# Cross-attention over eight batches: one addition of P1, one half's statistics and two sums of weights at other places of the order

## The chip, the core and the metric

The kernel runs on one core of a Trainium2 chip. The metric is device time in microseconds (us), the median of three runs. The engines are TensorE (PE in the profile, with PEld for its weight loads), VectorE (DVE), ScalarE (ACT), GpSimd (POOL) and SyncE (SP), which issues nearly all the transfers. Each engine works through its own queue in order.

## The reference, cut to what matters

Eight batches of 256 rows of 1024 numbers attend to 256 keys each, with 32 heads of 32 numbers. Keys and values are the same context.

```python
xn = (x - mean(x)) * rsqrt(var(x) + 1e-5) * gamma + beta
Q = heads(xn @ Wq.T); K = V = heads(ctx)
probs = softmax(where(mask, Q @ K.T / sqrt(32), -inf))
out = x + merge_heads(probs @ V) @ Wout.T
```

Everything is in float32.

## The kernel before, in words

**Slots.** The work is cut into 64 head groups, eight per batch, each of four heads. The main loop (from L937 on) has one pass per group; a pass is called a slot here. In slot n TensorE makes the scores of group n+1 (L963) and the products with the values of group n-2 (L973); VectorE, ScalarE and GpSimd make the softmax of group n+1 (`softmax_parts`, L512 to L618). So slot 9 holds the softmax of group 10. Beside these, each slot has a hand-placed share of other work.

**The softmax.** For each of four heads VectorE adds the mask to the scores and reduces them (L524), ScalarE takes the exponential and its sum (L528), VectorE makes the reciprocal (L535), GpSimd, VectorE or ScalarE scale by it (L543, L538), VectorE transposes the blocks (L549), ScalarE copies half of them aside (L555), and SyncE moves them into the tile pT (L614, L618). Points in the softmax take "hooks": evacuations of other products. The hook called "soon" comes behind the second head's reductions, hook 0 behind the fourth's.

**The output product.** Attention times Wout is done for batch b in slots 8(b+1) to 8(b+1)+8 by a Strassen-like scheme of seven half-size products: A11 by B11 (its result is called P1), A12 by B21, S2 by T2, S3 by T3, A22 by T4, S1 by T1, S4 by B22. Each has four steps of TensorE (L720; each step shows as two matmuls), given out by the table STEPS: in slot 9 seven steps, in slot 10 one behind the values and two behind the softmax, and so on; step 23, the last of S1 by T1, is the only one in slot 15 that comes right behind the values, and two more come later in that slot. A, the halves of the attention, are summed to S by GpSimd (`sum_at`, L696); the halves B of Wout are summed to T once, for all batches, chunk by chunk (`sum_wo`, L182). Accumulators are in PSUM: P1 in one bank, the sums that follow in another. ScalarE copies P1 out (`keep_p1`, L728). For each of the four quarters of the output GpSimd adds P1 to the residual r (`add_p1`, L753), and VectorE adds what stands in PSUM (`take`, L758, or `store`, L762, which also sends the result). The first quarter's store, r plus the result of A12 by B21, has to have read its bank before the S2 steps of TensorE begin in it.

**The query product.** Batches 0 and 1 make their queries directly; from batch 2 on (L447) there is the same scheme, with sums of the normalised x (`sum_x`, L435) and of Wq (`sum_wq`, L396: T1, T2, T3 and T4, each in four chunks, built once in slots 6 to 14). Batch 2's products stand in slots 10 to 16, one a slot: S1, S4, A11, S2 (with T2, slot 13), S3 (with T3), A22 (with T4, slot 15), A12. Batch 3's begin in slot 18.

**Layer norm.** For batch 3 the two halves of rows have their statistics (`ln_stats`: two BN statistics, L227, their aggregate, L230, and an addition, L232, on VectorE, then a power on GpSimd, L235) in slots 8 and 9, their normalisation (GpSimd's shift, L245, and ScalarE, L248) in slots 10 and 11, their block transposes (L316) in slots 11 and 12, and their moves by SyncE (L332) in slots 12 to 14. In slots above 8 the statistics come behind the softmax on VectorE, and the power is put off to a list called `later`.

**GpSimd's order in a slot** is: its parts of the softmax, S2's sum (when it is due), shift, the other sums of attention, sums of x, additions of P1 in slots 11 to 13, the powers of `later`, folds of Wq (early slots), and last `sums[n]`, the slot's sums of weights. In `sums[n]` the sums of Wout entered at L853 come first, then those of Wq (L858), then Wout's T1 (L860).

Of the kernel before, what the change touches and what calls it, by code (L numbers as in the profile page):

```python
# [59 lines left out]
def xattn_kernel(  # L60
# [101 lines left out]
    B11, B21, B22, T1, T2, T3, T4 = range(7)  # L162
# [201 lines left out]
    def fold(o):  # L364

        nc.gpsimd.tensor_tensor(
            wq[:, o], wq[:, o], gs.unsqueeze(2).to_broadcast([P, NC, P]), ALU.mult
        )
# [9 lines left out]
    SPLIT = 2  # L378
# [295 lines left out]
    def steps_of(b):  # L674
        if b == B - 2:
            return ENDS
        return STEPS
# [73 lines left out]
    def add_p1(b, s, h):  # L751
        r = rs[b, s, h]
        nc.gpsimd.tensor_tensor(r, r, p1s[b], ALU.add)  # L753
# [46 lines left out]
    for n in range(N):  # L800
# [12 lines left out]
    loads, stats, norms, trans, moves, biases, masks = (  # L813
        {n: [] for n in range(N)} for _ in range(7)
    )
    for b in range(1, B):
        first = NQ * (b - 1) + 2
        if b == 1:
            when = dict(moves=())
        elif b == 2:  # L820
            when = dict(
                loads=(0, 1), stats=(2, 3), norms=(3, 4), trans=(4, 5),
                moves=tuple(5 + (i + 2) // 6 for i in range(16)),
            )
        else:
            when = dict(
                loads=(first - 12, first - 11) if b == SPLIT + 1 else (first - 13, first - 12),
                stats=(first - 10, first - 9) if b == SPLIT + 1 else (first - 11, first - 9),
                norms=(first - 8, first - 7), trans=(first - 7, first - 6),
                moves=tuple(first - 6 + (i + 2) // 6 for i in range(16)),  # L830
            )
        for table, key in (
            (loads, "loads"), (stats, "stats"), (norms, "norms"), (trans, "trans"),
        ):
            for i, n in enumerate(when.get(key, ())):
                assert n < first
                table[n].append((b, i))
        for n in range(N):
            part = [i for i, slot in enumerate(when["moves"]) if slot == n]
            if part:  # L840
                assert n < first - 1
                moves[n].append((b, part))
        biases[NQ * b - 2].append(b)
        if b % 2 == 0:
            masks[NQ * b - 7].append(b)


    sums = {n: [] for n in range(N)}
    for n, which, *chunks in (
        (0, T3, 0), (1, T3, 1), (2, T2, 0), (3, T2, 1), (4, T3, 2, 3), (5, T2, 2, 3),  # L850
        (6, T4, 0, 1), (8, T4, 2), (11, T4, 3),
    ):
        sums[n] += [partial(sum_wo, which, c) for c in chunks]  # L853
    for n, which, *chunks in (
        (6, "T1", 0), (7, "T1", 1, 2, 3), (8, "T2", 0), (9, "T2", 1), (10, "T2", 2), (11, "T2", 3),
        (11, "T3", 0), (12, "T3", 1, 2), (13, "T3", 3), (13, "T4", 0), (14, "T4", 1, 2, 3),
    ):
        sums[n] += [partial(sum_wq, which, o) for o in chunks]  # L858
    for n, *chunks in (12, 0, 1), (13, 2), (14, 3):
        sums[n] += [partial(sum_wo, T1, c) for c in chunks]  # L860


# [33 lines left out]
    for c in range(NC):  # L896
        copy_x0(1, c, nc.scalar if c < NC // 2 else nc.vector)
    first = softmax_parts(0, (partial(copy_q, 1), partial(copy_q, 2)), (), (), {}, [
        partial(ln_stats, 1, 0), partial(ln_stats, 1, 1),
        partial(ln_norm, 1, 0, nc.vector),  # L900
    ])
# [16 lines left out]
    for b in range(B - 1):  # L918
        done, ends = 0, b == B - 2
        for i, counts in enumerate(steps_of(b)):  # L920
            n = NQ * (b + 1) + i
            for place, k in enumerate(counts):
                steps.setdefault((n, place), []).append((b, range(done, done + k)))
                done += k
        for i, *what in (
            ((2, keep_p1), (3, take_po_q), *((i, copy_po, i) for i in range(3, 8))) if ends else
            ((1, keep_p1), (2, add_p1, 0, 0), (2, store, 0, 0), (3, take, 0, 1), (4, take, 1, 1), (6, store, 1, 0),
             (7, store, 1, 1), (8, store, 0, 1))
        ):
            evacuations[NQ * (b + 1) + i].append((what[0], b, *what[1:]))  # L930
# [6 lines left out]
    for n in range(N):  # L937
        b, i = divmod(n - NQ, NQ)
# [109 lines left out]
            make_q(halves[n], second=True, chunks=range(NC // 2))  # L1048
        if n + 2 < NQ:
            fold(n + 2)  # L1050
        for one in sums[n]:
            one()
        if N - NQ + 2 < n < N - 1:
# [106 lines left out]
```

## Time and profile before

| what | us |
|---|---|
| median of three runs | 571.01 (570.69 to 571.02) |
| the profiled execution | 571.32 |
| its span, first to last instruction | 569.5 |
| TensorE busy | 561.8 |
| VectorE, ScalarE, GpSimd busy | 468.5, 423.7, 394.0 |

The granted TensorE clock is 1.00 throughout, and HBM gives and takes 137 GB/s over the span. The starts of slots, taken from the first score matmul of each in TensorE's timeline, are: slot 9 at 89.14, 10 at 97.50, 11 at 107.48, 12 at 116.84, 13 at 125.35, 14 at 133.86, 15 at 142.37, 16 at 152.26, 17 at 159.90, 18 at 168.27.

How to read it: a group's line gives the code line, the engine, the operation, out<-in, and a count. In a timeline the first two numbers are the start and the duration in us, and a bracket at the end gives the engine's idle time before the instruction and what ended it. In the waits view a line says who waited for whom, then the total in us, the number of waits and the longest. In the table by stretches a row gives the stretch, its length, each engine's busy time with its count of instructions, the granted clock, the DMA share and GB/s. The ends of matmuls are modelled, so starts are the firmer numbers.

### The profile page before, as it was taken

How to read it: one execution, taken by the hardware profiler on the slowest of the kernel's cores; microseconds unless marked ns; L12 is line 12 of the kernel's file. 1: busy time of each engine (PE TensorE's matmuls, PEld its weight loads, DVE VectorE, ACT ScalarE, POOL GpSimd, SP SyncE). 2: the span in 40 equal slices, each digit the busy share in tenths (PEclk: the TensorE clock that was granted, in tenths of full speed). 3: DMA queues.
4: the chain of work that ended last, by engine and by line, in shares of the span. 5: the costliest groups of instructions: out<-in, count | busy, mean ns of one | idle time of the engine just before them, and what ended most of it. 6: DMA issues, size and time to landing. Idle time of an engine off the chain costs nothing.

```text
span 569.5 us, 20200 instructions
## 1 busy us (share of the span) xinstructions
PE 561.8 (99%) x7266; PEld 393.9 (69%) x7266; DVE 468.5 (82%) x1716; ACT 423.7 (74%) x1464; POOL 394.0 (69%) x636
## 2 busy tenths in 40 slices
PE   8999999999999999999999999999999999999997
PEld 7888886667667777667776777667866767755454
DVE  5979889899888888979898888988888878779923
ACT  3699999898668858787667867778767776769920
POOL 2688887899687565866569566677648657448780
PEclk9999999999999999999999999999999999999999
DMA  8966677756798667867788857887658874536751
GB/s 306 397 174 204 179 199 223 252 176 174 219 305 247 202 177 198 289 203 214 195 243 227 226 166 211 261 246 202 185 142 253 251 202 133 146 103 182 216 157 74
DMA packets 47219, 119.02 MB, mean 209 GB/s; under 512 B 8976, under 2 KB 9744, under 8 KB 47120
## 3 DMA queue, kind: packets, MB, share of 16 engines
q1 hardware_dynamic: 46976, 117.74, 69.8%
q8 instruction: 57, 0.93, 0.8%
q14 instruction: 42, 0.34, 0.2%
q10 hardware_dynamic: 144, 0.01, 0.0%
HBM read 66.33 MB, written 11.53 MB: 137 GB/s over the span
## 4 chain that ended last, share of the span: by engine, by line
PE 80%; POOL 7%; DVE 5%; ACT 3%; issue 3%; DMA 1%; SPq 0%; DVEq 0%; POOLq 0%; ACTq 0%
PE po_S L720 20%; PE pq_A L447 18%; PE pv L636 10%; PE sc L486 10%; PE po_A L720 10%; PE pq_S L447 7%; PE po_end L787 3%; ACT e L528 2%; POOL e L543 2%; DVE e L524 2%; DVE pT L549 1%; PE po_last L787 1%; POOL wq L396 1%; POOL wo L182 1%; DMA pT<-pT 1%
## 5 line engine op out<-in xcount | busy, mean ns | idle before, releaser
L543 POOL TENSOR_SCALAR e<-e,rden 128x256 f32<-128x256 f32 x466 | 215.3, 478 | 128.7 <-DVE rden L535 126.1
L528 ACT ACTIVATE e<-e,mn 128x256 f32<-128x256 f32 x512 | 254.1, 502 | 47.4 <-DVE mn L524 46.3
L549 DVE STREAM_TRANSPOSE pT<-e 128x512 f32<-128x512 f32 x256 | 179.0, 704 | 35.6 <-POOL e L543 26.2
L524 DVE CUSTOM_DVE_ANT_0 e<-sc,mb 128x256 f32<-128x256 f32 x512 | 185.4, 416 | 27.0 <-PE sc L486 26.7
L555 ACT COPY pc<-pT 128x512 f32<-128x512 f32 x128 | 79.0, 617 | 55.2 <-DVE pT L549 34.9
L528 ACT ACTIVATION_READ_ACCUMULATOR e<-e,mn 128x1 f32 x512 | 98.6, 193 | 0.0
L486 PEld LDWEIGHTS sc<-k,qa 32*128 32x128 f32 x1024 | 46.2, 184 | 42.1 <-issue 20.1
L720 PE MATMUL po_S<-wo,at 128*128 128x512 f32 x152 | 74.3, 606 | 0.0
L636 PE MATMUL pv<-pT,v 64*32 64x128 f32 x4096 | 74.1, 274 | 0.0
L486 PE MATMUL sc<-k,qa 32*128 32x256 f32 x1024 | 73.6, 401 | 0.1
L636 PEld LDWEIGHTS pv<-pT,v 64*32 64x32 f32 x4096 | 57.0, 105 | 22.5 <-issue 12.4
L720 PE MATMUL po_A<-wo,at 128*128 128x512 f32 x128 | 59.4, 605 | 0.0
L345 PE MATMUL pq<-xnT,wq 128*128 128x256 f32 (+1 forms) x240 | 55.0, 384 | 0.0
L447 PEld LDWEIGHTS pq_A<-xnT,wq 128*128 128x128 f32 x416 | 48.5, 192 | 6.2 <-issue 5.0
L720 PE MATMUL po_S<-wo,s 128*128 128x512 f32 x104 | 50.2, 607 | 2.5 <-POOL wo L182 1.3
L345 PEld LDWEIGHTS pq<-xnT,wq 128*128 128x128 f32 x240 | 44.6, 190 | 8.2 <-issue 1.5
L447 PE MATMUL pq_A<-xnT,wq 128*128 128x128 f32 x416 | 48.5, 275 | 0.0
L535 DVE RECIPROCAL rden<-den 128x2 f32<-128x2 f32 x256 | 38.3, 150 | 7.7 <-ACT e L528 6.5
L524 DVE DVE_READ_ACCUMULATOR2_ANT mn<- 128x1 f32 x512 | 42.6, 83 | 0.0
L720 PEld LDWEIGHTS po_A<-wo,at 128*128 128x128 f32 x128 | 23.0, 190 | 25.6 <-issue 24.4
L720 PEld LDWEIGHTS po_S<-wo,at 128*128 128x128 f32 x152 | 25.5, 190 | 19.5 <-issue 19.5
L753 POOL TENSOR_TENSOR r<-r,p 128x512 f32<-128x512 f32 x24 | 30.6, 1275 | 5.0 <-DMA r<-in_x_dram 4.0
(102 smaller groups left out, 665.8 us busy)
## 6 DMA issues: line engine op xcount, KB each, us to landing
v<-in_kv_dram SPq DMA_DIRECT2D x32, 512.0 KB, 4.1
pT<-pT SPq DMA_DIRECT2D x128, 128.0 KB, 3.3
pT<-pc SPq DMA_DIRECT2D x128, 128.0 KB, 4.1
ring<-kept_T SPq DMA_DIRECT2D x20, 512.0 KB, 5.3
k<-in_kv_dram SPq DMA_DIRECT2D x32, 256.0 KB, 4.0
x<-in_x_dram SPq DMA_DIRECT2D x15, 512.0 KB, 5.9
r<-in_x_dram SPq DMA_DIRECT2D x28, 256.0 KB, 4.6
out_dram<-r SPq DMA_DIRECT2D x28, 256.0 KB, 3.5
```

The costliest lines, as they stand in the source:

```text
L345: nc.tensor.matmul(pqs[n], wq[:, o, c, :], xnTs[b](c), start=(c == 0), stop=(c == NC - 1),)
L447: nc.tensor.matmul(pqs[b][:, o, :], w[:, c], x_[:, c], start=begins and o + c == 0, stop=c == NK - 1, skip_group_check=True,)
L486: nc.tensor.matmul(scs[n][j][:, s, :], qa[r, n % NQ, ts(s, P)], ks[n - n % 2][r, n % 2, :], start=True, stop=True,)
L524: nc.vector.tensor_tensor_reduce(out=e[:, s, :], in0=pss[j][:, s, :], in1=mbs[n // NQ], scale=1.0, scalar=NO_SCORE, op0=ALU.add, op1=ALU.m ...
L528: nc.scalar.activation(e[:, s, :], e[:, s, :], AF.Exp, bias=mn[:, s : s + 1], scale=-1.0, accum_out=den[:, s : s + 1],)
L535: nc.vector.reciprocal(rden, dens[j])
L543: engine.tensor_scalar(es[j][:, s, :], es[j][:, s, :], rden[:, s : s + 1], 1.0, ALU.mult, ALU.mult,)
L549: nc.vector.transpose(pT[:, :, :, j, :, :].rearrange("p a i s k -> p (a i) s k"), es[j].rearrange("p s (b t) -> p b s t", t=K),)
L555: nc.scalar.copy(pc[:, :, ts(j, 2)], pT[:, 1, :, ts(j, 2)])
L636: nc.tensor.matmul(pvs[n][r][j * HD : (j + 1) * HD], vs[n - n % 2][ts(r, 2 * K), i, ds(n % 2 * P + j * HD, HD)], pT[ts(r, 2 * K), :, i, j, ...
L720: nc.tensor.matmul(po, operand(b, name)[:, c], wo[:, which, c], start=begins and c == 0, stop=c == NK - 1, skip_group_check=not begins,)
L753: nc.gpsimd.tensor_tensor(r, r, p1s[b], ALU.add)
```

## The change

```diff
-                stats=(first - 10, first - 9) if b == SPLIT + 1 else (first - 11, first - 9),
+                stats=(first - 10, first - 8) if b == SPLIT + 1 else (first - 11, first - 9),
...
+    sums[14].append(partial(sum_wo, T1, 3))
     for n, which, *chunks in (
-        (6, "T1", 0), (7, "T1", 1, 2, 3), (8, "T2", 0), (9, "T2", 1), (10, "T2", 2), (11, "T2", 3),
+        (6, "T1", 0), (7, "T1", 1, 2, 3), (8, "T2", 0), (10, "T2", 1, 2), (11, "T2", 3),
         (11, "T3", 0), (12, "T3", 1, 2), (13, "T3", 3), (13, "T4", 0), (14, "T4", 1, 2, 3),
     ):
         sums[n] += [partial(sum_wq, which, o) for o in chunks]
-    for n, *chunks in (12, 0, 1), (13, 2), (14, 3):
+    for n, *chunks in (12, 0, 1), (13, 2):
         sums[n] += [partial(sum_wo, T1, c) for c in chunks]
...
-            ((1, keep_p1), (2, add_p1, 0, 0), (2, store, 0, 0), (3, take, 0, 1), (4, take, 1, 1), (6, store, 1, 0),
+            ((1, keep_p1), *(((2, add_p1, 0, 0),) if b else ()), (2, store, 0, 0), (3, take, 0, 1), (4, take, 1, 1), (6, store, 1, 0),
...
         if n + 2 < NQ:
             fold(n + 2)
+        if b == 0 and i == 1:
+            add_p1(0, 0, 0)
         for one in sums[n]:
             one()
```

Four things move, and nothing is computed otherwise. For batch 3 (`first` is 18) the second half's statistics go from slot 9 to slot 10, with their power. Batch 0's first addition of P1 goes from the "soon" hook of slot 10 to the end of slot 9 in GpSimd's order, ahead of that slot's sums of weights. T2's chunk 1 of Wq goes from slot 9 to slot 10, in front of chunk 2. T1's chunk 3 of Wout stays in slot 14 and goes from behind T4's chunks 1 to 3 of Wq to in front of them.

## The prediction

> **What bounds the kernel now.** The first part of the page and the waits view, TensorE alone, carry the answer. The lines shown are the engine's busy time, and who TensorE waited for (total us, times, longest).
>
> ```profile
> PE 561.8 (99%) x7266; PEld 393.9 (69%) x7266; DVE 468.5 (82%) x1716; ACT 423.7 (74%) x1464; POOL 394.0 (69%) x636
> ```
>
> ```profile
> PE busy L119 <- POOL ring masks.py:199: 1.3, 1, 1.3
> PE po_S L720 <- POOL wo L182: 1.3, 1, 1.3
> PE po_S L720 <- DVE r L762: 1.2, 1, 1.2
> PE px L273 <- DVE ring L883: 0.8, 1, 0.8
> ```
>
> TensorE is busy for 99% of the span, and only two of its waits lie in the body of the kernel: one for VectorE's r (L762), one for GpSimd's wo (L182). So an edit pays only by removing these two, and the question is what each is really worth. The timeline of TensorE puts the first at 105.56 us (slot 10) and the second at 145.91 us (slot 15). The table by stretches gives both slots from their first score matmul to the next slot's (columns: length, then busy time of each engine), and beneath them slots 18 and 23, which do the same steps for the next batch without a wait:
>
> ```profile
> 97.50:107.48 9.98, 8.78 (x120) 6.25 (x119) 9.08 (x34) 7.33 (x26) 9.20 (x13) 1.00 0.94 319
> 142.37:152.26 9.89, 8.58 (x120) 6.25 (x119) 8.88 (x30) 7.22 (x25) 8.40 (x12) 1.00 0.84 252
> 168.27:176.78 8.51, 8.51 (x120) 6.25 (x119) 7.62 (x29) 6.37 (x24) 7.46 (x14) 1.00 0.88 266
> 211.73:220.25 8.52, 8.52 (x123) 6.25 (x122) 7.14 (x28) 6.70 (x25) 4.07 (x9) 1.00 0.69 198
> ```
>
> Slot 10 is 9.98 - 8.51 = 1.47 us too long, slot 15 is 9.89 - 8.51 = 1.38 us (slot 23 runs 211.67 to 220.18 by its starts, so 8.51). I count these differences, together 2.85 us, and not the two idle times (2.51 us), since the ends of matmuls are modelled. The Trainium skill says so too ("Perfetto Trace Analysis", section "Tensor Engine Instruction (MATMUL, LD_WEIGHTS)": the end is an estimate, the start is observed); by the idle column the gain would be 0.34 us less.
>
> **The addition of P1 (slot 10 to slot 9).** The chain of waits behind 105.56 is read from GpSimd's timeline (start, duration):
>
> ```profile
> 101.76 0.55 POOL L235 TENSOR_TENSOR rstd<-ve,mhalf 128x1 f32<-128x1 f32 x1
> 102.28 1.27 POOL L396 TENSOR_TENSOR wq<-wq,ring 128x512 f32<-128x512 f32 x1
> 103.50 1.28 POOL L753 TENSOR_TENSOR r<-r,p 128x512 f32<-128x512 f32 x1
> 104.75 0.94 POOL L543 TENSOR_SCALAR e<-e,rden 128x256 f32<-128x256 f32 x2
> ```
>
> and VectorE's:
>
> ```profile
> 104.82 0.69 DVE L762 TENSOR_TENSOR r<-po_A,r 128x512 f32<-128x512 f32 x1 [0.80 <-POOL r L753]
> ```
>
> TensorE's S2 steps need the bank that this store reads; the store needs the addition (L753); and in GpSimd's queue the addition stands behind the power of batch 3's second half (0.52 from start to start) and T2's chunk 1 (1.22). Both go behind it now. It starts when the sum before it ends, at 101.76, and ends 1.25 later, at 103.01: 1.74 us earlier. Its operands are there: P1 was copied by ScalarE from 97.47 to 98.05, and r, issued at 96.00, landed 3.0 us later. Even the slowest load of r in the trace, 5.9 us, would cost only 0.14.
>
> On VectorE the four instructions of the statistics (99.53 to 101.12, 1.59 us) leave their place ahead of slot 10's softmax. Its scores were ready by 98.65, so the softmax starts at 99.53 instead of 101.12, and its last score reduction ends near 102.4. The store then starts at 103.05 (102.4 is no longer the limit) instead of 104.82. TensorE's steps began 0.74 after the store's start; by that they may start at 103.79. TensorE itself is ready at 100.63 + 3.58 = 104.21 (3.58 is slot 18's spacing of the same 32 matmuls). The wait goes, with 0.42 us to spare: **1.47 us** gained. What is late next there is TensorE's own work. The store's transfer keeps its place in SyncE's queue (issued at 106.49, behind that of kept_B at 105.86), so no queue is passed.
>
> **The statistics in slot 10.** They add 1.59 us to VectorE behind that slot's softmax. From the store's start to the next softmax took 3.86 (104.82 to 108.68): 103.05 + 3.86 + 1.59 = 108.50, against 108.68 before. So VectorE is where it was, while TensorE is 1.47 earlier. The first user that this could hurt is in slot 11: VectorE's addition out of the S2 bank ran from 112.92 to 113.61, and TensorE wanted the bank at 115.03, now at 113.56. But ahead of it VectorE waited 1.30 us at 112.11 for ScalarE's sums, and ScalarE comes some 1.4 us earlier (it waited 1.38 for the reduction at 101.64). The wait goes, the addition ends near 112.3. I cost this edit at nothing; the cover is 1.2 us, a lag above it is paid one for one, and if the 1.30 stayed the cost would be 0.05. The result is needed only by the normalisation of the half in slot 11, whose shift ran at 115.63.
>
> **GpSimd in slot 10.** Its queue gets the power and T2's chunk 1 behind slot 10's sums. By the same spacings: two pairs of e, the shift and two sums end at about 108.3; the power waits for VectorE until about 108.5; then 0.52 + 1.24 + 1.24 end at 111.5, against 111.25 before. Behind it stands slot 11's e, which started at 112.44 after a wait of 1.16, so at worst it starts as late as before. T2's chunk 1 is first read by T3's chunk 1 (slot 12) and by TensorE in slot 13, 128.48. Cost: nothing. Here the skill has a rule that speaks against moving sums about ("SBUF — State Buffer", section "Who interferes with whom": VectorE and GpSimd lock their shared port pair against each other). The rows show the size: VectorE's two e of j=1 took 1.04 beside GpSimd's (95.84) and 0.62 alone (105.62). One such collision more is 0.42 us of VectorE, inside the cover of 1.2, so by the rows the sum stays; by the rule alone it could be 0.42 worse.
>
> **T1's chunk 3 of Wout, ahead of T4's.** GpSimd's rows in slot 14, and TensorE's in slot 15:
>
> ```profile
> 140.82 3.81 POOL L396 TENSOR_TENSOR wq<-wq 128x512 f32<-128x512 f32 x3
> 144.58 1.28 POOL L182 TENSOR_TENSOR wo<-wo 128x512 f32<-128x512 f32 x1
> ```
>
> ```profile
> 143.44 1.16 PE L636 MATMUL pv<-pT,v 64*32 64x128 f32 x64
> 145.91 1.13 PE L720 MATMUL po_S<-wo,s 128*128 128x512 f32 x2 [1.31 <-POOL wo L182]
> 146.87 3.73 PE L447 MATMUL pq_A<-xnT,wq 128*128 128x128 f32 x32
> ```
>
> Now the sum ends at 140.82 + 1.25 = 142.07 even if GpSimd comes no earlier. TensorE is ready at 143.44 + 1.09 - 1.47 = 143.06. T4's chunks end at 143.3, 144.6 and 145.86 instead of 142.1, 143.3 and 144.6. The product that reads them follows one step (0.96) later and takes a chunk every 0.89, so chunk 3 is needed at 143.06 + 0.96 + 2.68 = 146.70. Both are in time, by 0.99 and 0.84 us. **1.38 us** gained.
>
> **The sum.** 571.32 (profiled execution: span 569.5 and 1.8 around it) - 1.47 - 1.38 = 568.47. That execution lies 0.31 above the median of the three runs, 571.01, so I take 568.2.
>
> **Beyond slot 15** TensorE is 2.85 earlier and the others must follow. VectorE waited for scores at 153.42 (0.86), so it follows. SyncE's queue is the doubtful one: it waited for ScalarE's copies up to 135.38, then ran behind its own DMAs until about 167. The pT of head group 16 was sent from 160.71 (1.15 for two issues, 5.3 to land: 166.6 at the latest) and TensorE read it at 169.35. If SyncE comes 1.4 earlier, 1.3 us remain; if it doesn't at all, TensorE at 166.50 waits 0.1.
>
> **Rivals.**
> *One wait stays* (12%). The spare times are 0.42, 0.99 and 0.84 us, and each rests on estimates of where four engines come to stand. If VectorE's store still comes after 104.2, or GpSimd is 1 us later in slot 14, the time is 568.2 + 1.4 = 569.6. Against it: the addition's two operands and its place in the queue are known to 0.1 us.
> *Given back or nothing happens* (7%). A later wait, of SyncE's transfers or a bank's release by VectorE, eats 2 us or more, or the moved work makes both waits reappear: about 570.5, up to 571. For it: GpSimd is without a gap of 0.4 us from 114.73 to 145.86, VectorE is busy for some 96% of slots 12 to 14 (8.23, 8.12 and 8.15 of 8.51). Against it: batch 1's slots do the same steps with no TensorE wait.
> *Slower* (3%). GpSimd runs in order, and the power now stands in slot 10 ahead of T2's two sums and slot 11's e. A wait of w for VectorE makes GpSimd w later; its idle 2.51 in slot 11 and 0.76 up to slot 14 absorb 3.27, and the 0.84 of T4's chunk 3 the next. So it costs w - 4.1, passes the gain at w = 7.0 and is 0.2% slower at 8.1: about 572.5 for 8.5. The longest wait of that line anywhere in the trace is 6.3, which leaves 570.4.
>
> **Numbers.** Both waits go: 78%, 568.2, alone 567.7 to 568.8, which holds nine in ten of these cases. From 567.6 to 569.8 takes in the first rival too: about eight in ten of it all. Faster by over 0.2% (below 569.87; about what a measurement of this kernel can tell from no change) holds the forecast and nearly all of the first rival: 89%. Within 0.2%: 8%. Slower: 3%.
>
> **What would show it.** In the new profile no body wait of TensorE is left in the waits view; slots 10 and 15 are 8.5 us long; the addition starts at about 101.8 and the store at about 103.1; the power stands at about 108.5 with a short wait; the chunk of wo comes first in slot 14. I am wrong if TensorE waits for VectorE's r, for wo or wq in slots 10 to 16, or for pT near 166.

## The result and the profile after

The changed kernel takes 568.28 us in the median of six runs (567.80 to 569.33), the kernel before 570.90 (570.69 to 571.10) beside it: ratio 0.9957, 95% interval 0.9945 to 0.9970. The profiled execution took 567.81, with a span of 566.0. The kernel is faster by about what was forecast, but its six runs scatter over 1.5 us where the six of the kernel before scatter over 0.4, and that was not forecast. (In longer series the kernel before scatters over 0.95 us in 29 runs, the changed kernel over 1.7 in eleven.)

The page of the changed kernel: TensorE's busy time, and the chain that ended last by engine. On the page before the chain began with "PE 80%; POOL 7%; DVE 5%"; now nearly all of it is TensorE's.

```profile
PE 561.4 (99%) x7266; PEld 393.7 (70%) x7266; DVE 467.6 (83%) x1716; ACT 423.4 (75%) x1464; POOL 394.3 (70%) x636
...
PE 97%; DMA 1%; DVE 0%; POOL 0%; ACT 0%; issue 0%; SPq 0%; POOLq 0%
```

All that TensorE still waits for, in its own waits view of the changed kernel:

```profile
PE busy L119 <- POOL ring masks.py:199: 1.3, 1, 1.3
PE px L273 <- DVE ring L884: 0.2, 1, 0.2
```

Slots 10 and 15 in the table by stretches, changed kernel:

```profile
96.83:105.34 8.51, 8.51 (x120) 6.20 (x119) 7.81 (x31) 7.52 (x26) 7.72 (x11) 1.00 0.86 298
140.23:148.74 8.51, 8.51 (x119) 6.25 (x118) 7.48 (x28) 6.64 (x24) 7.77 (x12) 1.00 0.79 230
```

Both are 8.51 long, as slots 18 and 23 were, and TensorE is busy for all of it. So 1.47 + 1.38 = 2.85 us went there. Slot 10 also begins at 96.83 instead of 97.50: this execution was 0.67 earlier from the scores of slot 0 on (22.52 against 23.19), before any changed instruction, which the change cannot have done. 571.32 - 2.85 - 0.67 = 567.80, against 567.81: these three terms account for the difference of the two profiled executions to 0.01 us. GpSimd's rows of slots 9 and 10 in the changed kernel's timeline, then VectorE's store:

```profile
101.08 1.27 POOL L753 TENSOR_TENSOR r<-r,p 128x512 f32<-128x512 f32 x1
102.33 0.93 POOL L543 TENSOR_SCALAR e<-e,rden 128x256 f32<-128x256 f32 x2
...
108.00 0.55 POOL L235 TENSOR_TENSOR rstd<-ve,mhalf 128x1 f32<-128x1 f32 x1 [0.39 <-DVE ve L232]
108.53 2.50 POOL L396 TENSOR_TENSOR wq<-wq,ring 128x512 f32<-128x512 f32 x2
111.01 1.05 POOL L543 TENSOR_SCALAR e<-e,rden 128x256 f32<-128x256 f32 x2
```

```profile
102.39 0.69 DVE L762 TENSOR_TENSOR r<-po_A,r 128x512 f32<-128x512 f32 x1 [0.67 <-POOL r L753]
```

Add 0.67 to each to compare with the prediction's clock: the addition at 101.75 (forecast 101.76), the store at 103.06 (103.05), the power at 108.67 after a short wait (about 108.5), slot 11's first e at 111.68 (at worst 112.44).

In slot 14 GpSimd now makes the sum of Wout before T4's three chunks, and TensorE reads it in slot 15 without a wait (GpSimd's rows, then TensorE's):

```profile
138.53 1.27 POOL L182 TENSOR_TENSOR wo<-wo 128x512 f32<-128x512 f32 x1
139.77 3.79 POOL L396 TENSOR_TENSOR wq<-wq 128x512 f32<-128x512 f32 x3
```

```profile
142.40 1.12 PE L720 MATMUL po_S<-wo,s 128*128 128x512 f32 x2
```

### The profile page after: what moved, and what is told of

Read it like the earlier page. It is cut to its first block, busy times and chain, and to the rows that moved or that the text cites. A ratio compares the mean times of both kernels' runs of the same rounds, so it can differ in the third digit from the quotient of the medians.

```text
span 566.0 us, 20200 instructions
## 1 busy us (share of the span) xinstructions
PE 561.4 (99%) x7266; PEld 393.7 (70%) x7266; DVE 467.6 (83%) x1716; ACT 423.4 (75%) x1464; POOL 394.3 (70%) x636
## 4 chain that ended last, share of the span: by engine, by line
PE 97%; DMA 1%; DVE 0%; POOL 0%; ACT 0%; issue 0%; SPq 0%; POOLq 0%
PE po_S L720 21%; PE pq_A L447 19%; PE pv L636 12%; PE sc L486 12%; PE po_A L720 11%; PE pq L345 9%; PE pq_S L447 8%; PE po_end L787 3%; PE po_last L787 1%; DMA x<-in_x_dram 1%; PE po_end_s L787 0%; POOL x L885 0%; PE pq L290 0%; PE px L307 0%; ACT e L528 0%; PE px L273 0%
```

## The experiments

The first four runs take the change apart.

**Only the addition of P1 is moved.**

```diff
-            ((1, keep_p1), (2, add_p1, 0, 0), (2, store, 0, 0), (3, take, 0, 1), (4, take, 1, 1), (6, store, 1, 0),
+            ((1, keep_p1), *(((2, add_p1, 0, 0),) if b else ()), (2, store, 0, 0), (3, take, 0, 1), (4, take, 1, 1), (6, store, 1, 0),
...
+        if b == 0 and i == 1:
+            add_p1(0, 0, 0)
```

> Of the change only the addition of P1 is moved; the statistics, T2's chunk 1 and T1's chunk 3 stay. Theory (GpSimd's order sets both waits): in slot 9 the addition stands behind the power, so it ends 0.52 later than in the full change, and VectorE's store is held until the softmax behind the statistics is reduced: a wait of about 0.55 us is left in slot 10 (0.92 gained there). But GpSimd reaches T1's chunk 3 in slot 14 only some 0.5 earlier, so the wait in slot 15 grows to about 1.8, and the whole gain is only about 0.5 us: some 570.4. Rival (each wait is worth its own length wherever the other stands): 0.92 to 1.47 us gained, 569.4 to 570.0, and slot 15 as long as before.

Measured: 570.23 us (569.90 to 571.10, eleven runs) against 570.82: ratio 0.9990 (0.9981 to 0.9999), 0.6 us gained. Its timelines in slots 14 and 15, GpSimd and TensorE:

```profile
144.30 1.28 POOL L182 TENSOR_TENSOR wo<-wo 128x512 f32<-128x512 f32 x1
```

```profile
145.63 1.13 PE L720 MATMUL po_S<-wo,s 128*128 128x512 f32 x2 [1.53 <-POOL wo L182]
```

TensorE still waits for T1's chunk 3, and that chunk comes only 0.28 earlier than before. What is gained in slot 10 is mostly given back in slot 15, as the theory had it: slot 15 is 10.11 long, against 9.89 before, and the rival had it as long as before. The times alone are weaker, since the interval of the ratio reaches from 0.1 to 1.1 us gained and so into the rival's range. The wait of 0.55 in slot 10 was not seen in this trace, since slot 10 began late in this execution (98.27): slot 2's values had waited 0.96 us for pT.

**Only T1's chunk 3 is moved.**

```diff
+    sums[14].append(partial(sum_wo, T1, 3))
...
-    for n, *chunks in (12, 0, 1), (13, 2), (14, 3):
+    for n, *chunks in (12, 0, 1), (13, 2):
```

> Of the change only T1's chunk 3 of Wout is moved in front of T4's chunks. Theory: the wait of slot 15 goes and that of slot 10 stays at 1.2 in the idle column, 1.38 us gained, about 569.5. Rival (T4's chunk 3, now last, holds TensorE in slot 15): a wait for wq in place of that for wo, up to 1.2 us, about 570.7. On the scatter of the changed kernel's runs (567.8 to 569.3): if it comes from slot 10's wait coming back in some executions, this kernel, which always has it, scatters by no more than the kernel before (0.4); if it comes from elsewhere, it scatters by 1.5 too.

Measured: 569.46 (569.21 to 570.15), ratio 0.9978 (0.9969 to 0.9988): 1.36 us gained, 1.38 expected. In TensorE's waits view the line for wo is gone, none for wq has come, and slot 10's is as it was:

```profile
PE po_S L720 <- DVE r L762: 1.2, 1, 1.2
```

Its ten runs lie within 0.94 us: wider than the 0.4 of the one theory of the scatter, narrower than the 1.5 of the other, so this told nothing on that. (Twenty runs of the kernel before, taken with them, lie within 0.65.)

**All but the statistics.** The full change with this line as before:

```diff
-                stats=(first - 10, first - 8) if b == SPLIT + 1 else (first - 11, first - 9),
+                stats=(first - 10, first - 9) if b == SPLIT + 1 else (first - 11, first - 9),
```

> The full change but for the statistics, which stay in slot 9. Theory: the power stands ahead of the addition again (0.52) and the statistics ahead of slot 10's reductions on VectorE, so the store starts near 104.0 on the clock of the trace of before, not 103.05, and a wait of about 0.55 us stays in slot 10; slot 15 has none: 2.3 us gained, about 568.6. Rival 1 (the statistics' place doesn't matter, the 0.42 us of spare time covers it): the same as the full change. Rival 2 (it was VectorE's order all along that held the store): the whole 1.47 stays, about 569.5.

Measured: 568.82 (568.31 to 569.23), ratio 0.9961 (0.9948 to 0.9975), 2.0 us gained. Its lowest run is 0.5 above the lowest of the changed kernel's first series, as the theory had it, but its median lies between the medians of the changed kernel's two series (568.28, and 568.86 below). So the times do not show what the statistics are worth. Its trace cannot show the wait: slot 10 began 1.07 later than in the changed kernel's (97.90), which was late enough for the store. An estimate from the two traces supports the theory: here the store starts 4.40 after the statistics (99.31 to 103.71); in the changed kernel VectorE gets to that place at 98.84, so the store would start at 103.24 and TensorE, 0.74 behind it, at 103.98 instead of 103.53, which is a wait of 0.45.

**All but T2's chunk 1.** The full change with `(9, "T2", 1), (10, "T2", 2)` as before.

> The full change but for T2's chunk 1 of Wq, which stays in slot 9, now behind the addition. Theory: TensorE has neither wait, since the addition is already ahead of that sum; GpSimd's first e of slot 10 starts 1.2 later and VectorE's first transpose waits about 0.8 for it, which nobody waits for: the same as the full change within 0.3 us. Rival (the late e makes VectorE late in slots 10 to 12, and a bank's release with it): 0.4 to 1.2 us slower than the full change, with a TensorE wait for VectorE's r in slots 11 to 13.

Measured: 567.65 (567.62 to 568.05), ratio 0.9946 (0.9934 to 0.9959), no body wait of TensorE. GpSimd's first e of slot 10 starts 1.17 later than in the changed kernel (103.50, against 102.33), and VectorE's transpose waits 0.30 for it, with no consequence. So this part of the change is not needed for the gain.

The next three ask what the addition's own place is worth, and what lateness of TensorE costs.

**All but the addition.** The full change, with the addition left on slot 10's soon hook.

> The full change but for the addition of P1, which is issued from slot 10's soon hook as before. Theory (what counts is what stands ahead of the addition in GpSimd's queue, not the slot it is written in): the power and T2's chunk 1 are out of its way, so it follows the sum of x at once, as in the full change; both TensorE waits stay away and the time is that of the full change, 567.7 to 569.3. Rival (the addition's own place is what removes the wait): slot 10's wait of 1.2 us is back, about 569.5.

Measured: 568.31 (567.79 to 569.48), ratio 0.9950 (0.9937 to 0.9963). GpSimd's timeline, the sum of x and the addition behind it:

```profile
100.50 1.28 POOL L435 TENSOR_TENSOR sx<-sx,xnT 128x512 f32<-128x512 f32 x1
101.73 1.28 POOL L753 TENSOR_TENSOR r<-r,p 128x512 f32<-128x512 f32 x1
```

Nothing stands between them, though the code calls the addition a slot later. Slot 10 is 8.51 long here too. What matters is what is queued ahead: with the statistics and their power moved, either T2's move (this run) or the addition's (the run before) clears the way. The execution (569.48) had another wait, in slot 18: TensorE's line, then GpSimd's:

```profile
172.98 1.98 PE L720 MATMUL po_S<-wo,s 128*128 128x512 f32 x4 [0.71 <-DVE r L762]
```

```profile
170.93 1.27 POOL L753 TENSOR_TENSOR r<-r,p 128x512 f32<-128x512 f32 x1 [3.36 <-DMA r<-in_x_dram]
```

It is the same chain as slot 10's, one batch later: S2's steps behind the store, the store behind the addition, the addition now behind the landing of r, which SyncE had issued at 164.86. Counted by stretches, slot 18 is 9.48 us long, 0.97 more than 8.51. It is not the only such trace: slot 18 is 8.92 long in the run without the statistics' move and 8.70 in that with T1's chunk alone, each time with the steps 0.74 or 0.75 behind the store and the store behind an addition before which GpSimd had stood idle (2.70, where the profile names ScalarE's e as what ended it, and 2.57, where it names r's landing).

**Scores of slot 7 made twice,** in the kernel before and in the changed kernel. The expectations count this as 1.08 us more work for TensorE; in the traces slot 7 became 0.87 longer (8.41 in the changed kernel with the repeat, 7.54 without).

```diff
-    def scores(n, part=range(NS)):
-        if 0 in part:
+    def scores(n, part=range(NS), again=False):
+        if 0 in part and not again:
...
             scores(n + 1)
+        if n == 7:
+            scores(n + 1, again=True)
```

> The kernel before, with the score matmuls of slot 7 made twice into the same banks, which puts 1.08 us of work on TensorE ahead of slots 10 and 15. Theory (before the change the two waits set the time, by GpSimd's and VectorE's queues, and TensorE's own lateness is taken up by them): no more than 0.2 us slower, 570.8 to 571.1, with slot 10's wait some 1 us shorter. Rival (TensorE, busy for 99%, sets the time and its work adds up): 1.08 us slower, about 571.9.

> The changed kernel with the same repeated score matmuls in slot 7. Theory: with both waits gone nothing takes up TensorE's lateness, so the whole 1.08 us shows, lowest run about 568.9 where the changed kernel's lowest was 567.8. Rival (the changed kernel has a floor of its own from another queue): less than 0.5 us slower in the lowest run.

Measured: the kernel before with it 571.07 (ratio 1.0004, 0.9995 to 1.0012; eleven runs, 570.63 to 572.63), the changed kernel with it 569.52 (ratio to the kernel before 0.9975, 0.9967 to 0.9983; lowest 568.80, against 567.80 without). In the first, slot 10's wait has shrunk and slot 15's is whole:

```profile
PE po_S L720 <- POOL wo L182: 1.3, 1, 1.3
...
PE po_S L720 <- DVE r L762: 0.4, 1, 0.4
```

Slot 10's idle time went from 1.20 to 0.35, by just the 0.85 that slot 10 came later against GpSimd's addition (98.04 and 103.19, before 97.50 and 103.50). So before the change 0.87 us of TensorE's work cost 0.1 in the medians (571.07 against 570.98), although TensorE was busy for 99%; after it, the same work costs 1.0 between the lowest runs and between the two profiled spans (567.0 against 566.0), and 0.8 between the medians (569.52 against 568.74 in eleven runs). This is shown by both pairs of runs.

The last five runs are on the scatter. The traces so far show three things that differ from execution to execution: when TensorE's first product begins (9.11 to 9.91 us), when slot 2's values get their first pT, and when batch 1's first r lands.

**Half of Wout's first loads later.** The changed kernel, with the second halves of B12, B22 and B11 loaded in slots 1 and 3.

```diff
-    for which, pair in ((B12, 0), (B22, 0), (B11, 0), (B12, 1), (B22, 1), (B11, 1)):
-        load_wo(which, pair)
+    for which in (B12, B22, B11):
+        load_wo(which, 0)
...
+        if n in (1, 3):
+            between += [partial(load_wo, one, 1) for one in ((B12, B22) if n == 1 else (B11,))]
```

> The changed kernel with the second halves of three loads of Wout (B12, B22, B11) issued in slots 1 and 3 instead of ahead of the loop. In the traces the first pT transfer lands between 33.3 and 35.1 us, behind these loads, and slot 2's values begin between 36.6 and 38.2. Theory (the scatter of the changed kernel's runs, 567.8 to 569.3, is this landing): the transfer lands earlier, the values never wait, and all runs lie within 0.5 us at about 567.7. Rival 1 (the scatter has another origin): it stays at about 1.5 us. Rival 2 (the sums of Wout in slots 4 and 5 then wait for their loads): GpSimd late, 0.5 us or more slower than the changed kernel's lowest run.

Measured: 570.00 (569.28 to 571.43), ratio 0.9982 (0.9974 to 0.9991): slower than the changed kernel. The first pT did land early: SyncE issued the second pair at 28.41, against 33.52 in the changed kernel. But two moved loads went out at 43.20, between the two pairs of group 2's pT (40.90 and 44.24), and slot 4's values then waited:

```profile
53.77 1.46 PE L636 MATMUL pv<-pT,v 64*32 64x128 f32 x64 [1.84 <-DMA k<-in_kv_dram]
```

The profile puts this wait down to a load of k, but these products read pT and v, and v had been issued before the moved loads; that it was pT's second pair is concluded from this. The landing came earlier as the theory said, and a new wait cost more than it brought; neither rival had named that place.

**The changed kernel again.**

> The changed kernel once more, on the same chip as the next three, for its scatter. Theory (two landings that the waits used to hide now show: pT's first in slot 2, up to 0.9 us, and batch 1's first r, sent in slot 16 and added in slot 18, up to 0.9 us): lowest 567.7 to 567.9, highest about 569.3, median 568.0 to 568.5. Rival (the six runs on record were an accident): all within 0.4 us.

Measured: 568.86 (568.42 to 569.49), ratio 0.9963 (0.9950 to 0.9975). Lowest and median lie above what the theory had, and the rival's 0.4 us is wrong too. Over both series its eleven runs go from 567.80 to 569.49, median 568.74. The profiled execution (568.87) shows the wait in slot 2:

```profile
37.28 0.38 PE L636 MATMUL pv<-pT,v 64*32 64x128 f32 x2 [0.52 <-DMA pT<-pc]
```

With it and a second wait of 0.16, slot 3 begins at 44.30, against 43.15 in the first profile of the same kernel. That is nearly all that sets the two executions apart: from slot 10's first score to TensorE's last group of matmuls it is 462.62 us here and 462.67 there.

**All but T2's chunk 1, again.**

> The full change without the move of T2's chunk 1, again. Theory (that move is worth nothing, and the five runs of 567.6 to 568.1 were luck with the landings): the same lowest as the changed kernel within 0.2 us and the same scatter of 1 to 1.5 us. Rival (leaving the sum in slot 9 is better by itself): lowest and median 0.3 us or more below the changed kernel's.

Measured: 568.20 (567.67 to 568.46), ratio 0.9949 (0.9937 to 0.9962). Over both series the ten runs without this move go from 567.62 to 568.46 (median 567.87), the eleven of the full change from 567.80 to 569.49. The lowest of all differ by 0.18, as the theory said, but the scatter is narrower than it said, and the median is 0.87 lower; beside the changed kernel's five runs of the same series both lowest and median are 0.7 lower, which is what the rival forecast. The traces speak against the rival: from slot 10's first score to TensorE's last group it is 462.55 and 462.60 us in the two traces without the move, 462.67 and 462.62 in the two with it, so T2's place changes TensorE's time by 0.1 at most there. What makes the medians differ came before slot 10 in these traces, or was in executions that were not profiled; it stays open.

**Batch 1's first r issued in slot 12.**

```diff
+            if n == 12:
+                between.append(partial(load_res, 1, 0, 0))
-            if i < 4:
+            if i < 4 and n != 16:
```

> The changed kernel with batch 1's first load of r issued in slot 12 instead of slot 16. In one trace of the kernel without the addition's move, GpSimd waited 3.36 us for that r in slot 18 and TensorE 0.7 for the store behind it. Theory: slot 18's addition follows its queue at once, slot 18 never has a TensorE wait, the lowest run is as before (567.8), the highest falls by 0.7 to 0.9 to about 568.7. Rival (SyncE's queue is late for pT as well, so another wait takes its place, or the scatter is the start's alone): the same highest, 569.3.

Measured: 568.05 (567.76 to 568.40), ratio 0.9947 (0.9933 to 0.9960). The addition of slot 18 has no wait any more:

```profile
167.61 1.28 POOL L753 TENSOR_TENSOR r<-r,p 128x512 f32<-128x512 f32 x1
```

The highest run fell by 1.1 (569.49 to 568.40); the lowest is where it was in the first series (567.80), and 0.7 lower than in the second (568.42). That r's wait in slot 18 can cost up to 0.97 us and is gone here is shown by the traces. That it is what lowered these five runs is not shown: the changed kernel's second profile has no such wait of TensorE (slot 18 is 8.51 long), and the ten runs without T2's move never went above 568.46 with r issued in slot 16.

**The same, and B11's second half loaded in slot 3.**

> As the run before, and the second half of B11's load goes from ahead of the loop to slot 3, which takes 0.5 MB out of the way of pT's first transfer. Theory: that transfer lands about 1 us earlier, between 32 and 34 us, slot 2's values wait no more, and the scatter falls to about 0.5 us around 567.7, faster than both kernels. Rival (as with three loads moved, the load put later holds a later pT up): a TensorE wait of up to 1.8 us in slots 4 or 5, median above 568.5.

Measured: 567.85 (567.77 to 568.21), ratio 0.9946 (0.9934 to 0.9959), a scatter of 0.44. SyncE issued pT's second pair at 31.88, and slot 2's values did not wait. All five runs lie below all five of the changed kernel on the same chip: by the medians this version beats the kernel before by 3.1 us, and the changed one by 1.0 in that series, by 0.9 over its eleven runs. But the lowest run of the changed kernel is as low (567.80), and so is the median of the ten runs without T2's move (567.87), which load as the changed kernel does. So the moved loads can't be called the only way to the narrow scatter.

## Why the prediction was right, and where it was not

*The two waits and their sizes.* Right, and not by luck: counting a stretch against the same stretch of a later batch gave 2.85, and 2.85 is what went between the two profiled executions. The idle column (2.51) would have been 0.34 short.

*The addition.* Right to 0.01 us in its time and in the store's. But I wrote of the addition as the thing moved; the run without its move shows that the gain is from clearing the queue ahead of it. With the statistics moved, its own place in the code should count only if T2's sum stayed in front, which was not run.

*The statistics.* Their move frees the addition of the power and the store of the statistics ahead of the reductions; that this is worth about 0.5 us is an estimate (0.45) from two traces, and the medians do not show it. The cost on VectorE was nothing, as said: the addition out of the S2 bank began at 110.65, TensorE took the bank at 112.89.

*T2's chunk.* Costed at nothing; the lowest runs and the traces agree, the medians differ by 0.87 for a reason that no trace shows. The collision that I had allowed for, 0.42 us of VectorE, did not come as one: its pair of e took 0.62 in slot 10 as before, and over slots 10 to 14 these pairs took 4.55 against 4.28, 0.27 more, which TensorE never saw.

*T1's chunk 3.* Right: 1.36 measured alone, 1.38 forecast.

*The rival "one wait stays".* The three spare times held (in slot 10 TensorE began 0.40 after the earliest that the store allowed, 0.42 forecast); none of the traces shows the waits of slot 10 or 15 back in the changed kernel.

*The slower rival.* The power waited 0.39 us for VectorE, far from the 7.0 at which the gain would have been gone.

*Beyond slot 15.* This step looked at the wrong transfer. I named SyncE's queue as the doubtful one and looked at pT of head group 16 near 166 us, which stayed harmless. The transfer that turned critical is batch 1's first r: before the change its addition began at 171.48 and TensorE's S2 steps at 174.97, 3.49 later; in the changed kernel's first profile 2.34 are left of that (169.12 and 171.46), and the store is 0.28 from holding TensorE. In two traces with slot 15's wait gone the landing did hold it, for 0.97 and 0.19 us of slot 18, and in a third the addition did, for 0.41, where the landing is not named.

*The sum against the median.* I subtracted 2.85 from a median and took the start as given. A lateness of TensorE alone, such as slot 2's wait for pT, goes into the two waits of the kernel before, as the repeated scores show, and slot 18 had spare time there; the changed kernel shows both. In the traces of the full change and of its variants from the statistics on to the moved loads of r and B11 (without the repeat and the run with three later loads), TensorE's lateness at slot 10, which is slot 2's waits and a late first product, and slot 18's r add up to the differences of the profiled spans within 0.15 us. That they also make up the scatter of the runs without a profile is argued, not shown. So the kernel before lies within 570.53 to 571.48 in 29 later runs, while the changed kernel's lowest run gained 2.9 us (570.69 to 567.80) and its median in the second series 2.1 (570.97 to 568.86). The forecast of 568.2 fits the recorded median of 568.28, and that it fits so closely is in part luck: the eleven runs' median is 0.5 higher. The range, 567.6 to 569.8, held all of them.

## What to carry to other kernels

Size a wait by comparing its stretch with the same work where nothing waits, and follow it back through the queue: what stands ahead of the late instruction matters, not where that instruction is written. Two waits in a row on the same late engine are not worth their sum one at a time: the first one's gain is given back at the second until both go (between the lowest runs, most of the first cleared alone gave 0.6 us, the second alone 1.3, both 2.9). A high busy share does not say that an engine's work sets the time: 0.87 us more of TensorE's cost 0.1 while two short waits were left. When the last wait on the bounding engine is gone, look for what it had been hiding, above all transfers with no spare time, before believing a median.

## What the runs showed of the hardware that I had not expected

Programs that are alike up to slot 2 start differently from execution to execution: TensorE's first product of queries began between 9.06 and 9.91 us. Slot 3 of the changed kernel itself began at 43.15 in one execution and at 44.30 in another; over the runs with the same loads it began between 43.03 (without T2's move) and 44.64 (with the addition alone). A transfer of 128 KB of pT that lands in a median of 3.3 us over the kernel before took longer early on, behind loads of Wout of 0.5 MB each: SyncE issued the first pair at 26.02 in the changed kernel and could go on to the next pair, which writes where the first reads, only at 33.52. In the run with the addition alone it was 26.14 and 35.11, and 26.08 and 28.41 when three of those loads were out of the way.
